# One row table per bin for all passes: surplus rows go on into the next pass's slots, and keys of paired groups are computed a step earlier

## The chip, the core and the metric

The kernel runs on one NeuronCore of a Trainium2 chip. A core has a matrix engine (TensorE, PE in the profile; its weight loads are PEld), a vector engine (VectorE, DVE), a scalar engine (ScalarE, ACT), a general engine (GpSimd, POOL) and a queue for transfers (SyncE, SP). Each runs its own list of instructions in order and waits for the others by semaphores. Tiles lie in on-chip memory of 128 partitions (SBUF), products of PE in PSUM, and everything large in the device's DRAM. The metric is the device time of one execution, in microseconds.

## What is computed

The reference is a layer of a graph network with 12,500 nodes (N), 400,000 edges (E) and 128 features:

```
h   = relu(layernorm(x))                     # N x 128
hin = h @ W_in2f.T
Wij = smu(f @ W_f1.T + b_f1) @ W_f2.T + b_f2 # E x 128, from 20 edge attributes
Wij = Wij * edge_weight[:, None]
x_ij = hin[dst] * Wij                        # one message per edge
agg = segment_sum(x_ij, src, N)              # messages added up by node
out = x + smu(agg @ W_o1.T + b_o1) @ W_o2.T + b_o2
```

`smu(v)` is a smooth bend of v (a linear part and an erf part), done with a GELU table. The edges are sorted by `dst`, so a run of edges reads few rows of `hin`; `src` is random, so the sum by `src` is a scatter.

## The kernel before

**Tiles, groups, passes.** 128 edges make a tile, 4 tiles a group (`GRP`), 2 groups a super-tile. There are 782 groups, and a step of the main loop stands for one of them. The groups are cut into ten passes (`PARTS`, called epochs in the code). The nodes are cut into 98 bins of 128.

**A group's way.** PE makes the hidden layer (`hide`, line 918), ACT bends it (`bend`, 926), PE weighs it (`weigh`, 998 and 1000). PE gathers rows of `hin` with a one-hot matrix (`gather`, 954), ACT scales them by the edge weights (`take`, 973), and DVE multiplies both (`mix`, 1040, or 1031 for a paired group) into a message tile `ms`, of which there are nine. Beside it, the place of every message in its bin is counted: DVE marks bins (671 to 725), PE counts with triangular matrices (`count`, 752), DVE takes the maximum (`read`, 796) and writes the row numbers `ix` (`number`, 818). Then POOL sends the tile, one indirect DMA per 128 rows, to a table in DRAM (`scatter_rows`, 1110). A row has 128 values and a last one that says which node of the bin it is for; in the last value the round of the table is also written (`mark`, 1088), so that older rows left in a table don't count.

**Paired groups.** In some groups tiles 2 and 3 are matched with tiles 0 and 1, and a matched pair is written as one double row. `number` writes `key` (812); PE spreads the keys (`spread_keys`, 830), DVE compares (`match`, 838), PE ranks what is left over (`rank_left`, 848 and 849), DVE turns the ranks into a selection (`place_left`, 855 and 856), PE permutes (`permute`, 875) and ACT copies (898, 899). Left-over rows go out with a later group, the host (`bins`, lines 724 and 725; `number`, line 821).

**Tables and sums.** Each pass fills a table with a fixed number of slots per bin (`CAP`, a multiple of 128 that the largest bin is to fit into). While pass k fills its table, the table of pass k-1 is read back and summed: SP fetches two or more bins into `rw` (`fetch`, 1141), DVE builds one-hot selections (`choose`, 1155), PE multiplies block by block of 128 rows (`add`, 1168), and ACT or DVE adds the result into `agg` (1180, 1182). The blocks per bin are CAP/128: 6, 6, 6, 6, 5, 4, 3, 3, 2, 1, together 42. The sums begin seven steps into a pass (`LANDED`). Three DRAM buffers serve the ten tables in turn (`BUFS`). Before a buffer's first use its slots above a safe minimum (`ZMIN`) are set to zero by SP (`clear`, 226), spread over the pass in front: table 0 in the first 50 groups, table 1 in the rest of pass 0, table 2 in pass 1.

**Order.** The order of PE, DVE, ACT and SP is written out by hand in the main loop (`tc.manual_schedule`). A step holds, in this order: `send`, leftovers of a timetable, `number` of the next group, `weigh`, half of the sums (`parts`), `spread_keys`, `mix`, `permute`, `match`, `gather` and `take` for the step after, `hide`, `bend`, `take_pairs`, `count`, `pick_part`, `number_left`, `bins`, `read`, the other half of the sums, `rank_left` and `place_left`. `load` asks SP for a super-tile's inputs three super-tiles ahead. `chores` issues the clears and fetches of a step. If a bin overflows its table, a flag sends the kernel into a second, plain path at the end.

Of the kernel before, what the change touches and what calls it, by code (L numbers as in the profile page):

```python
# [9 lines left out]
F32 = mybir.dt.float32  # L10
# [22 lines left out]
PARTS = (59, 58, 58, 58, 47, 37, 27, 24, 16, 7)  # L33
EVERY = (3,) + (2.5,) * 7
UNPAIRED = 10
FIRST_PAIRED = 50
LATE_OF = 1, 3
LATE_FREE = 6
# [3 lines left out]
BUFS = 3  # L42
SIGMA = 4.6
ROW = P + 1
BIG = 2047.0
ZP = 128
ROUND = 12582912.0
NOBIN_ROW = float(1 << 17)
# [3 lines left out]
def gnn_kernel(  # L52
# [45 lines left out]
    CAP, ZMIN = [], []  # L98
    for a, n in eps_of:
        last_groups = UNPAIRED / (SUP // GRP)  # L100
        paired = n - last_groups if 0 < len(CAP) < len(eps_of) - 1 else 0
        if not CAP:
            paired = max(0, n - last_groups - FIRST_PAIRED / (SUP // GRP))
        late_one = len(CAP) >= len(eps_of) - SENT_LAST
        every = LATE_OF[1] / LATE_OF[0] if late_one else EVERY[len(CAP)]
        if late_one and paired:
            paired = n - LATE_FREE / (SUP // GRP)
        mean = (n + WIDER * paired / every) * SUP * P * P / N
        dev = SIGMA * math.sqrt((n + 2 * WIDER * paired / every) * SUP * P * P / N)
        CAP.append(math.ceil((mean + dev) / P) * P)  # L110
        ZMIN.append(max(0, math.floor((n * SUP * P * P / N - dev) / ZP) * ZP) if len(ZMIN) < BUFS else 0)
    assert all(c <= CAP[k % BUFS] for k, c in enumerate(CAP)) and (EPOCHS - 1) // BUFS < GRP
    Q = [c // P for c in CAP]
    ROWS = 2 * max(Q)
    SPAN = [ROWS // q for q in Q]
    assert all(NB * c + P + max(CAP) + 2 * int(BIG) < NOBIN_ROW and c < BIG - 1 for c in CAP)
# [8 lines left out]
    SPILL = P + int(BIG) + max(CAP)  # L125
    SPILLS = 3
    stores = [dram.tile([NB * CAP[k] + SPILLS * SPILL, ROW], F32, name=f"buf{k}") for k in range(min(BUFS, EPOCHS))]
    bufs = [stores[k % BUFS][0:NB * CAP[k], :] for k in range(EPOCHS)]
    wide = [stores[k % BUFS][0:NB * CAP[k] + SPILLS * SPILL, :] for k in range(EPOCHS)]
# [50 lines left out]
    bad = const.tile([P, 5 + 2 * EPOCHS], F32, name="bad")  # L180
# [27 lines left out]
    spot = const.tile([P, 2], F32, name="spot")  # L208
    drow = const.tile([P, SPILLS * EPOCHS], F32, name="drow")

    CB = 2
    zero = const.tile([ZP, CB * max(c - z for c, z in zip(CAP[:BUFS], ZMIN)) * ROW // ZP], F32, name="zero")
    cleans = [(b, n) for b, n in chunks(NB - 1, CB)] + [(NB - 1, 1)]

    def clear(k, c, engine):

        b, n = cleans[c]
        if b == NB - 1:
            m = CAP[k] * ROW // ZP
            rows = bufs[k][b * CAP[k]:(b + 1) * CAP[k], :].rearrange("(p s) r -> p (s r)", p=ZP)  # L220
            for o, w in chunks(m, zero.shape[1]):
                engine.dma_start(rows[:, o:o + w], zero[:, :w])
            return None
        m = (CAP[k] - ZMIN[k]) * ROW // ZP
        rows = bufs[k][b * CAP[k]:(b + n) * CAP[k], :].rearrange("(b c) r -> b c r", c=CAP[k])[:, ZMIN[k]:, :]
        return engine.dma_start(rows.rearrange("b (p s) r -> p b (s r)", p=ZP),
                                zero[:, :n * m].rearrange("p (b m) -> p b m", b=n))


# [119 lines left out]
    with tc.tile_pool(name="ld", bufs=4) as ld, \  # L349
# [213 lines left out]
        pair_no = {g: i for i, g in enumerate(list(paired) + late_pairs)}  # L563
        more_met = down.bitcast(F16)
# [123 lines left out]

        def bins(g):
# [21 lines left out]
            if g in first:  # L711
                nc.vector.memset(before, 0.0)
# [30 lines left out]
        def count(g):  # L743
# [17 lines left out]
            else:  # L761
# [4 lines left out]
                if lot is not None:  # L766
                    part(pc[:, n], tri, lot)
                    part(pc[:, n], ones_h, since[:, 2], stop=True)
# [1346 lines left out]
```

## Time and profile before

| | |
|---|---|
| median of three runs | 3832.49 us (3823.35 to 3832.53) |
| profiled execution | 3826.85 us |
| its span, first to last instruction | 3825.1 us |
| mean granted clock of TensorE | 0.964 |
| moved by DMA | 905.06 MB, 237 GB/s |

The page of the profile gives, for each engine, the time in which it was busy and its share of the span; a chain of waits, followed back from the last instruction; and groups of equal instructions, each with line, engine, operation, what it writes and reads, count, busy time, mean time of one, and the idle time of the engine in front of them with what ended it. Other views ask the same trace by line, by stretch of time, or by who waited for whom: there, "A <- B: t, n, m" says that A waited for B for t us in n cases, at most m at once. "issue" is time in which the engine waited for nothing that the profile shows. Stretches are given in us from the span's start; in each, the busy time of an engine has the count of its instructions behind it, followed by the granted clock, the busy share of the 16 DMA engines and GB/s.

### The profile page before, as it was taken

What the parts mean: (1) busy time and instruction counts of PE and PEld (TensorE: products, weight loads), DVE (VectorE), ACT (ScalarE), POOL (GpSimd) and SP (SyncE); (2) the same over time, 40 slices, a digit from 0 to 9 for tenths busy, and PEclk for the clock granted to TensorE, in tenths of its full rate; (3) what the DMA queues carried; (4) which work ended last, traced back from release to release, by engine and by line L of the source; (5) the groups of instructions that cost most, each with busy time, mean ns of one, the idle gap of its engine ahead of it and who ended that gap; (6) DMA issues with size and microseconds to landing.
All of it is one profiled execution on the core that took longest, in us unless ns stands there. A gap on an engine that the chain in (4) does not pass through costs nothing.

```text
span 3825.1 us, 90354 instructions
## 1 busy us (share of the span) xinstructions
PE 3294.2 (86%) x28066; PEld 2872.9 (75%) x28066; DVE 3116.8 (81%) x8275; ACT 2839.2 (74%) x7986; POOL 2855.5 (75%) x2946
## 2 busy tenths in 40 slices
PE   8777776988888999999989889999999889997767
PEld 4346665877777888878878778888888888887657
DVE  7878976877777888888888888888898888886657
ACT  7767766878888888888888888888778777875102
POOL 6777777777767777777777777777777777777776
PEclk9989988999999999999999999999999999999889
DMA  5888888888888878888878878888888888886977
GB/s 156 231 236 239 236 230 233 248 251 246 263 253 232 238 227 231 244 239 235 229 222 232 235 214 242 253 239 247 232 244 249 233 235 246 241 236 177 312 247 228
DMA packets 663936, 905.06 MB, mean 237 GB/s; under 512 B 179875, under 2 KB 462631, under 8 KB 663321
## 3 DMA queue, kind: packets, MB, share of 16 engines
q1 hardware_dynamic: 556025, 666.99, 63.5%
q0 software_dynamic: 100112, 219.93, 17.8%
q10 hardware_dynamic: 7312, 12.29, 0.9%
q8 instruction: 228, 3.74, 0.4%
q14 instruction: 259, 2.12, 0.2%
HBM read 500.66 MB, written 398.23 MB: 235 GB/s over the span
## 4 chain that ended last, share of the span: by engine, by line
PE 33%; DMA 18%; DVE 16%; ACT 11%; issue 11%; POOL 9%; SPq 2%; ACTq 0%; DVEq 0%; POOLq 0%
DMA buf<-ms,ix 12%; PE pg L1168 10%; POOL buf L1110 9%; PE pw L998 6%; PE pt L875 5%; ACT hg L973 3%; PE pc L752 3%; DVE se L1155 3%; DVE mt L838 2%; DVE ms L1040 2%; ACT oh L634 2%; ACT ge L926 2%; PE ph L954 2%; PE pw L1000 1%; DVE pc L796 1%
## 5 line engine op out<-in xcount | busy, mean ns | idle before, releaser
L1110 POOL DMA_INDIRECT buf<-ms,ix x2516 | 2444.3, 971 | 813.6 <-issue 569.0
L1168 PE MATMUL pg<-se,rw 128*128 128x128 f32 x8036 | 1168.7, 284 | 107.8 <-DVE se L1155 61.2
L1168 PEld LDWEIGHTS pg<-se,rw 128*128 128x128 f32 x8036 | 1037.2, 194 | 166.4 <-issue 65.5
L973 ACT ACTIVATE hg<-ph,w_sb 128x128 f32<-128x128 f32 x2784 | 781.9, 361 | 94.5 <-PE ph L954 80.4
L998 PE MATMUL pw<-w_f,ge 128*128 128x128 f32 x5568 | 779.2, 284 | 30.5 <-DVE ms L1040 14.3
L998 PEld LDWEIGHTS pw<-w_f,ge 128*128 128x128 f32 x5568 | 697.5, 197 | 50.0 <-issue 23.7
L1155 DVE TENSOR_TENSOR se<-irow_ps,rw 128x1536 f32<-128x1536 f32 (+1 forms) x345 | 587.4, 1703 | 112.1 <-DMA rw<-buf 89.5
L634 ACT ACTIVATE oh<-rbc,nrow 128x512 bf16<-128x512 uint8 x725 | 538.6, 743 | 33.5 <-DMA rbc<-rel_dram 33.1
L635 ACT ACTIVATE oh<-oh,onesb 128x512 bf16<-128x512 bf16 x743 | 536.0, 721 | 24.2
L796 DVE TENSOR_REDUCE pc<-pc 128x4 f32<-128x392 f32 (+1 forms) x782 | 466.4, 596 | 81.0 <-PE pc L752 77.4
L1040 DVE TENSOR_TENSOR ms<-pw,hg 128x512 f32<-128x512 f32 x482 | 330.2, 685 | 137.8 <-DMA buf<-ms,ix 36.5
L875 PE MATMUL pt<-ms,mt 128*128 128x129 f32 x2676 | 345.0, 279 | 55.0 <-DVE at L855 48.2
L875 PEld LDWEIGHTS pt<-ms,mt 128*128 128x128 f32 x2676 | 319.1, 193 | 66.7 <-issue 23.3
L752 PE MATMUL pc<-eo,tri 128*128 128x392 f16 x782 | 261.5, 334 | 69.8 <-DVE ix L818 46.8
L954 PE MATMUL ph<-hw,oh 126*128 126x128 bf16 x2784 | 274.4, 221 | 39.0 <-ACT hg L973 36.0
L926 ACT ACTIVATE ge<-pu 128x512 f32<-128x512 f32 x451 | 272.9, 605 | 17.4 <-PE pu L918 15.5
L752 PE MATMUL pc<-so,ones_h 128*128 128x392 f16 (+1 forms) x996 | 279.4, 306 | 0.1
L1000 PE MATMUL pw<-wls,f 128*128 128x128 bf16 x2784 | 274.2, 222 | 0.0
L1088 ACT ACTIVATE ms<-lo_b,mark 128x4 f32<-128x4 uint8 x309 | 91.3, 295 | 231.9 <-DVE ms L1040 219.7
L1110 POOL DMA_INDIRECT buf<-lt,ix x214 | 203.3, 950 | 78.0 <-issue 27.7
L954 PEld LDWEIGHTS <-oh 126*128 126x128 bf16 x2784 | 217.0, 99 | 52.5 <-issue 44.3
L752 PEld LDWEIGHTS <-ones_h 128*128 128x128 f16 x1554 | 151.8, 98 | 139.2 <-issue 17.1
(344 smaller groups left out, 5313.0 us busy)
## 6 DMA issues: line engine op xcount, KB each, us to landing
rw<-buf SPq DMA_DIRECT2D x292, 774.0 KB
f<-f_parts SPq DMA_DIRECT2D x370, 240.0 KB
buf<-zero SPq DMA_DIRECT2D x146, 387.0 KB
rbc<-rel_dram SPq DMA_DIRECT2D x389, 128.0 KB
buf<-ms,ix POOLq DMA_INDIRECT x2516
f_parts<-hs SPq DMA_DIRECT2D x105, 360.0 KB
rw<-buf SPq DMA_DIRECT2D x49, 645.0 KB
f_parts<-hs SPq DMA_DIRECT2D x107, 240.0 KB
```

The lines of the kernel that those rows point to most:

```text
L634: nc.scalar.activation(oh, loaded[s][1][:, o:o + n], AF.Abs, bias=pneg if s < FEW // SUP else nrow)
L635: nc.scalar.activation(oh, oh, AF.Relu, scale=-1.0, bias=onesb[:, 0:1])
L752: nc.tensor.matmul(to, by, of, start=start, stop=stop, skip_group_check=True)
L796: nc.vector.tensor_reduce(sl[:, :n], pc[:, :n], op=ALU.max, axis=AX.X)
L875: nc.tensor.matmul(po[:, j * (ROW + 1):j * (ROW + 1) + w], pp[:, o:o + P], ms[:, i, ROW:ROW + w], start=(i == 0), stop=(i == 1))
L954: nc.tensor.matmul(ph[:, j * P:(j + 1) * P], oh[:3 * WIN, a:a + P], hw[:3 * WIN, g % PER, :], start=True, stop=True)
L973: nc.scalar.activation(hg[:, j * P:(j + 1) * P], rows_of[g][:, j * P:(j + 1) * P], AF.Copy, scale=w_sb[:, t + j:t + j + 1])
L998: nc.tensor.matmul(pw[:, a:a + P], ge[:, a:a + P], w_f2, start=(a == 0), stop=False, skip_group_check=True)
L1040: nc.vector.tensor_tensor(ms[:, :n, 0:P], pw.rearrange("p (j f) -> p j f", f=P)[:, :n], hg.rearrange("p (j f) -> p j f", f=P)[:, :n], op=A ...
L1110: i = nc.gpsimd.indirect_dma_start(out=(wide if g in host or g in pair_no else bufs)[k][:, :], out_offset=bass.IndirectOffsetOnAxis(ap=ix, ...
L1155: nc.vector.tensor_tensor(se[:, a:a + n], own.unsqueeze(1).to_broadcast([P, n, P]), rows_in[c][:, a:a + n, P:P + 1].to_broadcast([P, n, P] ...
L1168: nc.tensor.matmul(pgs[0][:, g, :], rows_in[c][:, o, 0:P], sel[c][:, o, :], start=(q == 0), stop=(q == Q[k] - 1))
```

## The change

1. **One table for all passes.** Each bin has one stretch of S = 3200 rows in one DRAM tile, `store`. Pass k writes at `OFF[k]` in it. Passes 0 to 4 form a chain of five tables, 5 to 7 one of three, 8 and 9 stand alone (`CHAINS`). A bin that has more rows than `CAP[k]` goes on into the slots of the next pass's table, up to `LIM[k]`, and the next pass starts its counts with that surplus (`carry`, formed by a product with `one_h` at the end of a pass). Only the last table of a chain must hold the largest sum. The blocks per bin become 5, 5, 5, 5, 5, 4, 3, 3, 2, 1, together 38. The passes get other lengths (`PARTS`).
2. **Clears.** All five tables of the first chain are cleared above `ZMIN`, each in the first three quarters of the pass in front (`by_group`), from 64 partitions in place of 128. Pieces are at most three rows of 64 partitions and two bins, so tables 3 and 4 take two pieces where the others take one. Chains 2 to 4 lie over tables already read.
3. **Waits.** The dependences between scatters, fetches and clears are declared by hand: a pass's first fetch waits for all its scatters; scatters wait for the clears of the tables of their own and earlier passes, and, past three quarters of a pass, for those of the next; pass 5 waits for the fetches of tables 0 to 2.
4. **Keys.** `number` of a paired group moves from the start of the step before its `mix` to the end of the step in front, right after `read`.
5. **Ranks.** `spot` is negated and added on PE by a product with `ident` in `rank_left`; `place_left` compares the sum in PSUM with `falling`, a row of negative numbers, and line 855 falls away. In `bins`, two operations of a host become one, and its count uses `rest_h`.
6. Two kinds of message tile replace views of one; in `mix`, ACT's copy of keys is written after DVE's product.

```
-PARTS = (59, 58, 58, 58, 47, 37, 27, 24, 16, 7)
+PARTS = (58, 55, 54, 53, 48, 42, 33, 25, 16, 7)
+CHAINS = (5, 3, 1, 1)
-SIGMA = 4.6
+SIGMA = 4.5
-ZP = 128
+ZP = 64
...
+    for i, n in enumerate(CHAINS):
+        a = len(CAP)
+        ends = [0]
+        for k in reversed(range(a, a + n)):
+            ends.insert(0, max(ends[0] + 1, math.ceil(sum(rows_for(k, a + n)) / P)))
+        caps = [(u - v) * P for u, v in zip(ends, ends[1:])]
...
+    store = dram.tile([NB + SPARE, S, ROW], F32, name="buf")
+    rows_at = store.rearrange("b s r -> (b s) r")
...
+        z = 0 if b == NB - 1 else ZMIN[k]
+        m = (CAP[k] - z) * ROW // ZP
+        rows = store[b:b + n, OFF[k] + z:OFF[k] + CAP[k], :].rearrange("b (p s) r -> p b (s r)", p=ZP)
+        out = []
+        for o, w in chunks(m, zero.shape[1] // n):
+            out.append(engine.dma_start(rows[:, :, o:o + w], zero[:ZP, :n * w].rearrange("p (b m) -> p b m", b=n)))
+        return out
...
             if g in first:
-                nc.vector.memset(before, 0.0)
+                if carried(first[g]):
+                    nc.vector.tensor_scalar(before, carry, BIG, None, op0=ALU.min)
+                else:
+                    nc.vector.memset(before, 0.0)
...
-                    nc.vector.tensor_scalar(lot, bin_row, left_of[host[g]][1], None, op0=ALU.is_equal)
-                    nc.vector.tensor_add(then, whole, lot)
+                    lot = then
+                    nc.vector.scalar_tensor_tensor(then, bin_row, left_of[host[g]][1], whole, op0=ALU.is_equal, op1=ALU.add)
...
+                if carried(k + 1):
+                    on_one = bank_of[:, 1, :NB]
+                    nc.tensor.matmul(on_one, one_h, after, start=True, stop=True)
+                    nc.vector.tensor_scalar(carry, on_one, -float(CAP[k]), 0.0, op0=ALU.add, op1=ALU.max)
...
-            nc.tensor.matmul(at_, tri, met_of(g, 0, 2), start=True, stop=False, skip_group_check=True)
+            nc.tensor.matmul(at_, ident, spot, start=True, stop=False, skip_group_check=True)
+            nc.tensor.matmul(at_, tri, met_of(g, 0, 2), start=False, stop=False, skip_group_check=True)
...
-            at_ = cnt.tile([P, 2], F32, name="at")
-            nc.vector.tensor_tensor(at_, spot, kt[:, 2 * P:2 * P + 2], op=ALU.subtract)
             nc.vector.tensor_tensor(pp[:, 4 * P:].rearrange("p (j e) -> p j e", j=2),
-                                    irow_ps.unsqueeze(1).to_broadcast([P, 2, P]),
-                                    at_.unsqueeze(2).to_broadcast([P, 2, P]), op=ALU.is_equal)
+                                    falling.unsqueeze(1).to_broadcast([P, 2, P]),
+                                    kt[:, 2 * P:2 * P + 2].unsqueeze(2).to_broadcast([P, 2, P]), op=ALU.is_equal)
...
+                for j in range(FIRST):
+                    if (j == 0 and g >= BY) or 0 < j <= k or (j == k + 1 and is_clean(g)):
+                        behind_all(i, after_clear[j])
+                    else:
+                        apart(i, f"cleared{j}")
...
+        by_group = {k: eps_of[k][0] * PER + eps_of[k][1] * PER * 3 // 4 for k in range(FIRST - 1)}
...
-            elif k + 1 < BUFS:
+            elif k + 1 < FIRST and cleared < len(cleans):
                 past = BY if k == 0 else 0
-                upto = min(len(cleans), -(-(i + 1 - past) * len(cleans) // (ng - 4 - past)))
+                upto = min(len(cleans), -(-(i + 1 - past) * len(cleans) // (by_group[k] - g0 - 2 - past)))
                 while cleared < upto:
-                    clear(k + 1, cleared, nc.sync)
+                    cleared_rows(k + 1, cleared)
                     cleared += 1
...
             step()
-            number(at(p + 1))
+            if at(p + 1) not in paired:
+                number(at(p + 1))
             weigh(at(p + 1))
...
             read(at(p + 2))
+            if at(p + 2) in paired:
+                number(at(p + 2))
             parts(hi)
```

More of the change, by code (lines that the diff above doesn't have):

```diff
@@ L97, in gnn_kernel @@
     EPOCHS = len(eps_of)
[L98 to L111, printed above, removed]
@@ L1073, in send @@
             t, n = groups[g]
[L1074 removed]
+            ms = message_tile()
             places_in(g, ms)
@@ new lines, in gnn_kernel, with is_clean, behind_all, apart @@
+        sent = [[] for _ in range(EPOCHS)]
+        after_clear = [[] for _ in range(FIRST)]
+        after_fetch = [[] for _ in range(EPOCHS)]
+        def is_clean(g):
+            k = epoch[g // PER]
+            return k + 1 < FIRST and g > by_group[k]
+        def behind_all(i, names):
+            for name in names:
+                tc.add_manual_dep(i.ins, name, AFTER, reason="rows of a table")
+            names.clear()
+        def apart(i, others):
+            tc.declare_no_dep(i.ins, group=others, reason="slots are disjoint")
```

166 lines of the change are left out of this document (98 added, 68 removed).

## The prediction

> **What bounds the kernel now.** The page's busy shares come first. They put TensorE (PE) ahead and GpSimd (POOL) only level with the rest, and the chain of waits gives POOL 9%:
>
> ```profile
> PE 3294.2 (86%) x28066; PEld 2872.9 (75%) x28066; DVE 3116.8 (81%) x8275; ACT 2839.2 (74%) x7986; POOL 2855.5 (75%) x2946
> PE 33%; DMA 18%; DVE 16%; ACT 11%; issue 11%; POOL 9%; SPq 2%; ACTq 0%; DVEq 0%; POOLq 0%
> ```
>
> Both mislead here. POOL does one thing, the scatters of line 1110, and the groups by form and the instructions of that line show its real load:
>
> ```profile
> L1110 POOL DMA_INDIRECT buf<-ms,ix x2516 | 2444.3, 971 | 813.6 <-issue 569.0 <-DMA buf<-ms,ix 54.0 <-ACT ms L1090 39.9
> L1110 POOL DMA_INDIRECT buf<-lt,ix x214 | 203.3, 950 | 78.0 <-issue 27.7 <-DVE ix L821 16.6 <-DVE pc L796 4.6
> L1110 POOL DMA_INDIRECT buf<-ms,ix_kept x163 | 158.3, 971 | 49.7 <-issue 45.7 <-DMA buf<-ms,ix_kept 2.1 <-ACT ms L898 0.3
> L1110 POOL DMA_INDIRECT buf<-ge,ix x9 | 8.8, 979 | 2.7 <-issue 1.8 <-DMA w_sb<-in_x 0.3 <-ACT ms L1806 0.3
> ...
> L1110 POOL DMA_INDIRECT buf<-ms,ix x2516: 952/958/1520, 13.0 to 3544.0; - x194
> L1110 POOL DMA_INDIRECT buf<-ms,ix_kept x163: 954/958/1352, 3545.2 to 3763.6; - x163
>   issue: 644.3, 2111
> ```
>
> 2902 scatters take 2814.7 us. Ahead of each lies a gap that waits for nothing, 644.3/2111 = 0.305 us; for all, 885 us. Begun at 13.0, such a run without any other wait ends at 13.0 + 2814.7 + 885 = 3713. The last scatter begins at 3763.6 and so ends near 3764.5. **POOL loses only some 52 us to waits in the whole run**; behind it lies a tail of 61 us to the span's end, 3825.1. Where the 52 us lie, POOL's waits show, asked for 0 to 100, 100 to 600, 600 to 680 and 680 to 1200 us, then for 1200 to 3500. Below them stand the engines' busy times in stretches of 500 us, and the product that line 782 makes at the end of each pass:
>
> ```profile
> POOL buf L1110 <- ACT ms L1078: 7.7, 12, 2.2
> ...
> POOL buf L1110 <- ACT ms L1090: 14.5, 15, 3.4
> ...
> POOL buf L1110 <- DVE ix L821: 6.9, 2, 4.7
> ...
> POOL buf L1110 <- ACT ms L1090: 22.7, 14, 5.1
> POOL buf L1110 <- DVE ix L821: 7.6, 4, 4.0
> ...
> POOL buf L1110 <- ACT hg L973: 13.2, 42, 0.6
> ...
> L782 PE MATMUL ph<-so,ones_h x10: 203/203/242, 595.5 to 3674.4; 128*128 128x98 f16 x10
> ```
> ```profile
> core 0: us, PE busy (x) PEld busy (x) DVE busy (x) ACT busy (x) POOL busy (x), PEclk, DMA share, GB/s
> 100.00:600.00 500.00, 365.09 (x2489) 264.49 (x2488) 411.44 (x1265) 350.69 (x1001) 371.72 (x379) 0.90 0.83 233
> 700.00:1200.00 500.00, 434.57 (x3824) 387.79 (x3823) 390.42 (x1045) 408.94 (x1166) 364.29 (x376) 0.97 0.88 253
> 1200.00:1700.00 500.00, 457.42 (x4108) 407.71 (x4107) 427.84 (x1142) 431.20 (x1236) 380.15 (x394) 1.00 0.83 235
> 1700.00:2200.00 500.00, 452.01 (x4017) 403.06 (x4015) 422.24 (x1137) 424.48 (x1194) 379.77 (x393) 0.99 0.81 229
> ```
>
> With the gap of 0.305 taken off each, the five named waits are 4.0, 9.9, 6.3, 18.4 and 6.4 us, 45 in all: 14 in pass 0, which ends with the first product of line 782 at 595.5 us, and 31 in pass 1. From 1200 us on POOL runs scatter behind scatter, 394 and 393 in 500 us. **From there no work taken off PE, DVE or ACT moves the end.** The change can win what POOL loses before 1200 us, and scatters that fall away.
>
> **The change, part by part.**
>
> *Scatters.* Each paired group makes three scatters of four. By the code's rule 224 groups are paired in place of 223, since the passes have other lengths: 2901 scatters, 0.970 + 0.305 = 1.3 us gained.
>
> *Blocks, 42 to 38 per bin.* Tables 0 to 3 lose one each (6 to 5), summed in passes 1 to 4; tables 4 to 9 keep theirs.
>
> ```profile
> L1168 PE MATMUL pg<-se,rw 128*128 128x128 f32 x8036 | 1168.7, 284 | 107.8 <-DVE se L1155 61.2
> L1155 DVE TENSOR_TENSOR se<-irow_ps,rw 128x1536 f32<-128x1536 f32 x292 | 511.0, 1750 | 107.3 <-DMA rw<-buf 87.7 <-PE pg L1168 18.9 <-DMA rbc<-rel_dram 0.3
> L1155 DVE TENSOR_TENSOR se<-irow_ps,rw 128x1280 f32<-128x1280 f32 x49 | 72.6, 1482 | 4.8 <-PE pg L1168 2.8 <-DMA rw<-buf 1.8
> ```
>
> Two records make one block product, so a block costs PE 1168.7/4018 = 0.291 us. 98 bins lose 28.5 us in each of passes 1 to 4, 114 in all; DVE's selections lose 49 x 0.268 = 13 us a pass. In passes 2 to 4 this only makes PE wait longer for free message tiles. In pass 1 it falls on the path.
>
> *Keys at the end of the step in front.* The spreading transposes wait for line 812 (whole run, then 700 to 1200 us):
>
> ```profile
> PE pt L830 <- DVE key L812: 70.9, 63, 6.3
> ...
> PE pt L830 <- DVE key L812: 10.9, 9, 6.3
> ```
>
> The key is moved on DVE ahead of the second part of the sums and of place_left, which begin 0.16 us later; on PE up to 10.9 us fall away in pass 1. What is late next is the match, which then waits for its own transposes.
>
> *Smaller work on DVE, a product more on PE.*
>
> ```profile
> L724 DVE TENSOR_SCALAR el<-mv,lat 128x98 f16<-128x98 f32 x214 | 65.5, 306 | 0.3
> L725 DVE TENSOR_TENSOR so<-so,el 128x98 f16<-128x98 f16 x214 | 45.5, 213 | 7.3
> L1843 DVE SCALAR_TENSOR_TENSOR so<-mv,lat,so 128x98 f16<-128x98 f32 x8 | 2.6, 321 | 0.3
> L855 DVE TENSOR_TENSOR at<-spot,pt 128x2 f32<-128x2 f32 x214 | 32.0, 150 | 4.6 <-PE pt L849 4.0
> L849 PE MATMUL pt<-met,ones_h 128*128 128x1 f16 x192 | 31.3, 163 | 0.0
> ```
>
> Lines 724 and 725 become one form that line 1843 shows (0.519 to 0.321 us), and line 855 goes (0.150 us): 0.35 us for a paired group, 12 us of DVE in pass 1's 35. For it PE gets ident by spot, a float32 product of two columns that the trace doesn't show. Two records of L1168's rate (0.145) are 0.29 us, two of its mean (0.284) 0.57; I take 0.33, two of L849, as nearest in width: 11 us in pass 1. It can start before the match ends. The f16 row in place of the PSUM row in the comparison of line 856 I take at no change. The extra checks and the carry are a few operations of line 855's size, once or twice a pass.
>
> PE in pass 1 then loses 28.5 + 10.9 - 11 = 28 us (20 to 39), about the 31 that POOL lost there.
>
> *Clears and loads.* Tables 0 to 2 clear 192 rows of a bin, not 384; tables 3 and 4, new, 256 each, all written within the first three quarters of a pass, in 64-partition pieces, and for tables 3 and 4 two pieces per pair of bins. SP issues 349 clears in place of 149:
>
> ```profile
> L226 SPq DMA_DIRECT2D buf<-zero x147: 377/447/3212, 47.4 to 1139.6; - x147
> ```
>
> Bytes, with rows of 516: a table's clear over 98 bins falls from 19.6 to 9.9 MB in passes 0 and 1, and passes 2 and 3 get 13.1 each where they had none; fetches lose 6.5 MB in each of passes 1 to 4. Pass 1 moved 253 GB/s against 235 after it (the stretches above). Pass 2 lasts 399 scatters of 1.275 = 509 us, its clearing part 382; there it rises by 13.1 MB/382 us = 34 less 12 of the fetches, to 257 GB/s. Pass 1 falls by some 9 and 12 to 232: **what pass 1 bore moves there.**
>
> *New waits on POOL.* The first scatter past three quarters of a pass waits for the next table's clears, with all later scatters behind it. They are issued two groups earlier, SP runs ahead by three super-tiles of loads, and POOL lags: I take zero. If that cover is gone it costs up to four landings; the longest in the chain of waits is the first row here, the second is DVE's, in order of time:
>
> ```profile
> 142.84 10.55 DMA buf<-zero
> ...
> 645.90 1.76 DVE L1155 TENSOR_TENSOR se<-irow_ps,rw 128x1536 f32<-128x1536 f32 x1 [8.58 <-DMA rw<-buf]
> ```
>
> The second is the start of the sums in pass 1: the first fetch lands late, DVE stands 8.58 us, and POOL's 6.3 us follow. The change leaves this order, though the last quarter of pass 0 is now free of clears.
>
> **Sum.** Pass 1: of some 10 us at its start (6.3 and a wait of 4) I take 5 back, of the other 21 I take 15. Pass 0: 0, from -5 to +5, since its clears have half the bytes but a table's 49 now go out in 35 groups, not 64. Passes 2 and 3: 5 us of new waits, since the transfers are as dense as in old pass 1 while PE has less to do. Together -5 - 15 + 5 - 1.3 = -16 us. The profiled execution took 3826.85 us, 1.75 beyond its span and 5.6 below the median of the three runs, 3832.49. From the median: **3816 us**; this case's own range is 3800 to 3824.
>
> **Rivals.**
>
> *All waits go.* If pass 1 was bound by PE alone, the 45 us go and the new passes stay covered: 3832.5 - 46 = 3786. For it: 28 us less on PE there. Against it: the late first fetch, and transfers on the chain. It is also where a reader of the chain, who counts 114 us of products and 70.9 of key waits, is stopped by POOL. Chance 0.12.
>
> *No change.* Pass 1 waits for loads rather than PE. Loads stand in 700 to 1200 us thus:
>
> ```profile
> ACT oh L634 <- DMA rbc<-rel_dram: 11.1, 5, 7.0
> PE pu L918 <- DMA f<-f_parts: 5.5, 1, 5.5
> ```
>
> If these, and not PE, emptied the message tiles, halved clears return some 8 us and passes 2 and 3 take 5 of them: 3828. The clock could do the same: granted 0.90 at 100 to 600 us beside 365 us of PE, 1.00 at 1200 to 1700 beside 457. If less work in pass 1 brought it from 0.97 to 0.94, PE's 435 - 28 = 407 us there would grow by 13 and give back half. The Trainium skill, "TensorE: Matmul & The Clock Gate", section "What's actually happening", states that an idle window of about 3.4 us halves the clock; by that rule thinner work favours this rival, but the trace has 1.00 beside an idle PE of 43 us in 500, so I give it little. Chance 0.25.
>
> *Slower: SP falls behind in passes 2 and 3.* SP is one queue for clears, fetches and every load. Its waits are its slack (700 to 1200 us, then 1200 to 1700):
>
> ```profile
> SPq L1141 <- PE pg L1168: 19.5, 6, 5.9
> ...
> SPq L1141 <- PE pg L1168: 53.3, 19, 6.0
> SPq L1141 <- PE pt L849: 13.2, 7, 3.9
> SPq L604 <- ACT oh L634: 13.1, 11, 6.5
> ```
>
> At least 79.6 us of 500 without clears, 61 in the 382 us in which a pass clears. 99 clears of 0.447 us fit (44 us). Beyond 61/99 = 0.62 us each they don't. At 1.0 us, loads run 38 us late in each pass, and with the 21 us won before: 3832.5 - 21 + 76 = 3888 at worst, 3858 if the nine message tiles absorb 15 in each. For it: clears up to 3.212 us. Against it: they are half as large, and PE is lighter. The Trainium skill, "DMA: Bandwidth & Descriptors", section "Rules for kernel authors", asks for large transfers over all partitions, and calls those under 64 KB mostly overhead; the one-row pieces, 66 KB from 64 partitions, are what it warns of. No run yet shows such a piece. Chance 0.12.
>
> *The tables overflow.* Then the flag sends the kernel into its slow second path, and the time leaves this scale. The limits keep 4.5 deviations: chance 0.01.
>
> **How the numbers follow.** Forecast 0.50, all gone 0.12, no change 0.25, slower 0.12, overflow 0.01. A measurement tells about 0.3% (11.5 us) from no change. Below 3821 lie four fifths of the forecast and all of the first rival: 0.52. Within 0.3%: a tenth of the chances from the forecast, nearly all of no change: 0.35. Slower: 0.13. For 8 in 10 the range runs from 3786 to 3844.
>
> **What would show it.** Right: POOL's busy time in 700 to 1200 us at 378 or more, line 830 without key waits, 7252 records of line 1168 in place of 8036, and the last scatter 16 us sooner with the same tail. Wrong: waits of POOL above 0.3 us beyond 1200 us, SP's waits near zero in passes 2 and 3, POOL waiting for a clear, or a tail that changes. If POOL's gap or scatter time itself moved, the floor would.

## The result, and the profile after

The changed kernel takes **3854.93 us** (median of four runs, 3851.51 to 3856.58) beside 3831.08 us before (3823.35 to 3832.53): 1.0068 times the time before, 95% interval 1.0055 to 1.008. It is 0.7% slower, where 16 us less were forecast. The profiled execution took 3854.62 us with a span of 3852.9, 27.8 more than before.

The page's busy shares and chain, the scatters by form, and the instructions of their line (duration in ns, lowest, median and highest; first and last start in us). Line 1110 is now line 1133:

```profile
PE 3262.0 (85%) x27445; PEld 2856.5 (74%) x27758; DVE 3012.7 (78%) x7859; ACT 2814.7 (73%) x7992; POOL 2870.3 (74%) x2946
PE 31%; DMA 21%; DVE 18%; ACT 10%; issue 10%; POOL 9%; SPq 2%; DVEq 0%; ACTq 0%; POOLq 0%; another core or an unknown queue 0%
```
```profile
L1133 POOL DMA_INDIRECT buf<-ms,ix x2514 | 2456.1, 977 | 836.5 <-issue 549.8 <-DMA buf<-ms,ix 53.7 <-ACT ms L1113 41.4
L1133 POOL DMA_INDIRECT buf<-lt,ix x215 | 205.6, 956 | 69.3 <-issue 30.3 <-DVE ix L849 5.7 <-DVE so L736 4.3
L1133 POOL DMA_INDIRECT buf<-ms,ix_kept x163 | 158.8, 974 | 49.7 <-issue 45.1 <-DMA buf<-ms,ix_kept 3.1 <-DMA rw<-buf 0.6
...
L1133 POOL DMA_INDIRECT buf<-ge,ix x9 | 8.5, 941 | 2.7 <-issue 2.1 <-DMA rw<-buf 0.3 <-ACT agg L1255 0.3
```
```profile
L1133 POOL DMA_INDIRECT buf<-ms,ix x2514: 953/962/1941, 13.2 to 3572.9; - x194
...
L1133 POOL DMA_INDIRECT buf<-ms,ix_kept x163: 955/961/1442, 3574.1 to 3792.6; - x163
```

Less is busy on PE and DVE, as the change meant, and the span is longer all the same. The prediction's own sum tells where. 2901 scatters now take 2829.0 us, and with the gap of 0.305 each a run without other waits would end at 13 + 2829 + 885 = 3727; it was 3713. The last one ends at 3793.6, so POOL loses 67 us, not 52. The tail behind it stays (59.3, was 60.6). Of the 28 us more, **14 are dearer scatters and 15 are waits**.

The waits have moved. POOL's, asked for 360 to 600 and for 1200 to 2100 us, and the engines' busy times by stretches:

```profile
POOL buf L1133 <- issue: 50.3, 122, 4.0
POOL buf L1133 <- ACT ms L1113: 8.4, 5, 4.9
POOL buf L1133 <- ACT rw L289: 4.6, 1, 4.6
...
POOL buf L1133 <- issue: 151.8, 465, 3.7
POOL buf L1133 <- ACT ms L1113: 27.8, 17, 4.0
...
POOL buf L1133 <- DVE ix L849: 6.9, 11, 1.7
```
```profile
100.00:600.00 500.00, 375.15 (x2591) 278.20 (x2591) 413.44 (x1260) 357.01 (x1024) 364.13 (x367) 0.90 0.75 201
700.00:1200.00 500.00, 434.49 (x3776) 390.21 (x3828) 381.69 (x1009) 412.52 (x1183) 380.15 (x394) 0.96 0.85 238
1200.00:1700.00 500.00, 429.71 (x3727) 383.71 (x3778) 384.14 (x1004) 399.74 (x1151) 366.75 (x377) 0.97 0.86 235
1700.00:2200.00 500.00, 436.23 (x3838) 388.85 (x3890) 400.79 (x1047) 405.68 (x1166) 367.08 (x379) 0.98 0.88 242
```

POOL waits longer for late message tiles (line 1113) in pass 0, and between 1200 and 2100 us, where none of its waits had been longer than 0.7 us. The two rows `issue`, which name nobody, hold 13 and 10 us beyond 0.305 for each gap. Twelve of their gaps are longer than 0.5 us, and in eleven of these the scatter starts 0.75 us after DVE's product in `mix` (line 1063) has ended, so they are late message tiles as well. POOL's busy time in 700 to 1200 us rose from 364 to 380, back to back; in 1200 to 2200 it fell from 380 to 367 in each 500 us. The transfers did not get as dense there as forecast: 235 and 242 GB/s, where 257 were expected.

The next rows are the clears, the first row of SP's waits in 1200 to 1700 us, and ACT's wait in the whole run for the loads of `rbc`, from which it makes the one-hot matrix `oh` of the gather. This last wait was 33.1 us in 14 cases before:

```profile
L237 SPq DMA_DIRECT2D buf<-zero x349: 485/652/2812, 48.0 to 2035.5; - x175
```
```profile
SPq L1200 <- PE pg L1227: 15.7, 9, 3.9
...
ACT oh L644 <- DMA rbc<-rel_dram: 93.5, 37, 9.4
```

A clear now has at most half the bytes and takes 0.652 us to issue in place of 0.447. SP's first row there was 53.3 us; all rows of the view together fall from 115 to 51 us, and in 1700 to 2200 us from 120 to 37. So SP still waits now and then, but it has much less to spare, and what it loads comes late.

### The profile page after: what moved, and what is told of

Read it like the earlier page. It is cut to its first block, busy times and chain, and to the rows that moved or that the text cites. A ratio compares the mean times of both kernels' runs of the same rounds, so it can differ in the third digit from the quotient of the medians.

```text
span 3852.9 us, 89322 instructions
## 1 busy us (share of the span) xinstructions
PE 3262.0 (85%) x27445; PEld 2856.5 (74%) x27758; DVE 3012.7 (78%) x7859; ACT 2814.7 (73%) x7992; POOL 2870.3 (74%) x2946
## 4 chain that ended last, share of the span: by engine, by line
PE 31%; DMA 21%; DVE 18%; ACT 10%; issue 10%; POOL 9%; SPq 2%; DVEq 0%; ACTq 0%; POOLq 0%; another core or an unknown queue 0%
DMA buf<-ms,ix 14%; POOL buf L1133 9%; PE pg L1227 7%; PE pw L1025 6%; PE pt L902 5%; ACT hg L1000 3%; PE pc L767 3%; DMA rbc<-rel_dram 3%; DVE mt L866 2%; DVE pc L824 2%; DVE ms L1063 2%; DVE se L1214 2%; ACT oh L644 2%; PE pw L1027 2%; PE ph L981 1%
## 5 line engine op out<-in xcount | busy, mean ns | idle before, releaser
L1227 PE MATMUL pg<-se,rw 128*128 128x128 f32 x7252 | 1087.1, 286 | 109.0 <-DVE se L1214 61.7
L1227 PEld LDWEIGHTS pg<-se,rw 128*128 128x128 f32 x7252 | 954.2, 195 | 164.6 <-issue 59.1
L1025 PE MATMUL pw<-w_f,ge 128*128 128x128 f32 x5568 | 788.7, 286 | 44.6 <-DVE ms L1063 27.3
L1214 DVE TENSOR_TENSOR se<-irow_ps,rw 128x1280 f32<-128x1280 f32 (+1 forms) x345 | 535.4, 1552 | 128.3 <-DMA rw<-buf 101.9
L644 ACT ACTIVATE oh<-rbc,nrow 128x512 bf16<-128x512 uint8 x726 | 540.2, 744 | 93.5 <-DMA rbc<-rel_dram 93.5
L902 PE MATMUL pt<-ms,mt 128*128 128x129 f32 (+1 forms) x2688 | 356.0, 284 | 45.4 <-DVE mt L883 19.8
L902 PEld LDWEIGHTS pt<-ms,mt 128*128 128x128 f32 x2688 | 328.8, 197 | 58.4 <-issue 23.9
L953 ACT ACTIVATE ge<-pu 128x512 f32<-128x512 f32 x450 | 273.5, 608 | 16.7 <-PE pu L945 16.3
L767 PE MATMUL pc<-so,ones_h 128*128 128x392 f16 x782 | 261.2, 334 | 0.0
L681 DVE TENSOR_TENSOR eo<-irow_ps,ed 128x784 f16<-128x784 f16 (+1 forms) x391 | 216.9, 555 | 25.9 <-ACT ed L671 25.6
L1027 PEld LDWEIGHTS <-f 128*128 128x128 bf16 x2784 | 222.0, 101 | 9.8
```

What stands on the lines that cost most here:

```text
L644: nc.scalar.activation(oh, loaded[s][1][:, o:o + n], AF.Abs, bias=pneg if s < FEW // SUP else nrow)
L767: nc.tensor.matmul(to, by, of, start=start, stop=stop, skip_group_check=True)
L902: nc.tensor.matmul(po[:, j * (ROW + 1):j * (ROW + 1) + w], pp[:, o:o + P], ms[:, i, ROW:ROW + w], start=(i == 0), stop=(i == 1))
L1025: nc.tensor.matmul(pw[:, a:a + P], ge[:, a:a + P], w_f2, start=(a == 0), stop=False, skip_group_check=True)
L1027: nc.tensor.matmul(pw[:, a:a + P], fb[:, o + a:o + a + P], wls, start=False, stop=(a + P == n), skip_group_check=True)
L1214: nc.vector.tensor_tensor(se[:, a:a + n], own.unsqueeze(1).to_broadcast([P, n, P]), rows_in[c][:, a:a + n, P:P + 1].to_broadcast([P, n, P] ...
```

## The experiments

For each run with a comparable profile this table gives what the scatters of its trace show, in us: how much longer than 0.305 the gaps between scatters were, by stretch of the span, and the mean duration of a scatter. It is worked out as the prediction's sum was, from start and end of every scatter; there is one profile for each kernel. Every ratio below is to the kernel before on the same chip.

| | 0-600 | 600-1200 | 1200-2200 | waits in all | mean scatter | span |
|---|---|---|---|---|---|---|
| before | 19.6 | 31.3 | 0.7 | 52 | 0.9699 | 3825.1 |
| after | 31.0 | 0.2 | 36.3 | 67 | 0.9752 | 3852.9 |
| keys and ranks alone | 20.2 | 28.9 | 0.8 | 50 | 0.9749 | 3835.4 |
| tables alone | 26.5 | 0.0 | 28.3 | 55 | 0.9716 | 3829.4 |
| clears from ACT | 40.2 | 0.0 | 63.5 | 104 | 0.9728 | 3882.5 |
| half clears, old tables | 95.7 | 64.3 | 6.2 | 166 | 0.9712 | 3941.4 |
| whole clears | 24.1 | 1.0 | 0.6 | 26 | 0.9737 | 3807.4 |
| whole clears, old keys | 21.5 | 0.9 | 4.2 | 27 | 0.9742 | 3810.2 |
| whole clears, old keys and ranks | 18.3 | 0.0 | 0.0 | 18 | 0.9739 | 3800.2 |
| whole clears, old ranks | 16.7 | 0.8 | 0.0 | 17 | 0.9746 | 3801.3 |

Some runs fell on chips on which the kernel before itself took some 5650 us (medians of 5647 to 5716), with POOL waiting in every stretch; their times say little of this bound, and they stand together below.

### The two halves of the change

Keys and ranks alone, with the one operation for a host, on the tables of before:

```
-            number(at(p + 1))
+            if at(p + 1) not in paired:
+                number(at(p + 1))
...
+            nc.tensor.matmul(at_, ident, spot, start=True, stop=False, skip_group_check=True)
...
-            at_ = cnt.tile([P, 2], F32, name="at")
-            nc.vector.tensor_tensor(at_, spot, kt[:, 2 * P:2 * P + 2], op=ALU.subtract)
```

> The kernel before with the keys at the end of the step in front, the ranks with the added product, and one operation for a host; tables, clears and blocks stay as before. Theory Q (the loss comes from the many clears that SP issues, and from scatters 5 ns dearer, both belonging to the new tables): POOL's stalls in pass 0 and beyond 1200 us stay as before (20 and 1 us), the mean scatter stays at 0.970 us, and of the 31 us of stalls in pass 1 some 10 to 25 go: 3806 to 3821 us. Rival K (the moved keys or the ranks delay something in passes 0, 2 and 3): the eight stalls of pass 0 and those of 1200 to 2100 us appear here too: 3850 us or more. Rival B (pass 1 was eased by the lighter sums or the halved clears, not by the keys): stalls in pass 1 stay near 31 us: 3826 to 3832.

Measured: 3833.72 us, 1.0002 (0.9986 to 1.0018). Pass 1 keeps its waits, 28.9 of 31.3: this is rival B, to within 2 us. Neither the loss of rival K nor the gain hoped for from the keys is there.

The tables alone, with keys and ranks as before (the same lines, undone in the changed kernel; the one operation for a host stays):

> The changed kernel with the keys and the ranks of before; tables, clears and blocks as changed. Theory Q: the stalls of pass 0 and passes 2 and 3 are all here, and pass 1 keeps part of its stalls: 3855 to 3875. Rival K: without the moved keys the stalls go: 3815 to 3830. If the lighter sums and clears alone ease pass 1, 600 to 1200 us shows less than 10 us of stalls here too.

Measured: 3842.98 us, 1.0036 (1.0023 to 1.0049). The lighter sums and the clears of pass 1 end all its waits by themselves, and the new waits in pass 0 and in 1200 to 2200 us are here. Theory Q's places hold; its time was set too high, since keys and ranks turn out to cost, not to win: the change with them is at 1.0068.

### Who issues the clears, and in what pieces

```
-            for i in clear(k, c, nc.sync):
+            for i in clear(k, c, nc.scalar):
```

> The changed kernel with the clears issued by ScalarE's queue in place of SP's; the same pieces, the same bytes. Theory Q: SP gets 228 us (349 of 0.652) back, its waits return to 50 us or more in 1200 to 1700 us, and the 60 us of stalls of POOL in pass 0 and in passes 2 and 3 fall below 25, unless ACT, busy 80%, cannot bear 65 us more in a pass: 3800 to 3830. Rival D (the bytes of the clears crowd the loads, whoever issues them): stalls stay, 3850 to 3860. The mean scatter stays at 0.975 us by both.

Measured: 3891.94 us, 1.0167 (1.0137 to 1.0197), slower than both theories expected. The rows are the clears, SP's first wait and POOL's wait for the tiles in 1200 to 1700 us, and ACT's wait for `rbc` in the whole run:

```profile
L237 ACTq DMA_DIRECT2D buf<-zero x349: 477/583/2042, 50.2 to 2062.2; - x175
```
```profile
SPq L1200 <- PE pg L1227: 64.8, 20, 7.8
...
POOL buf L1133 <- ACT ms L1113: 31.6, 19, 4.2
...
ACT oh L644 <- DMA rbc<-rel_dram: 5.4, 3, 3.5
```

With the very same pieces `rbc` is waited for 5.4 us in place of 93.5, and SP has its slack again. This row alone doesn't settle why, since ACT, which waits for `rbc`, is late itself here. The loads' own time does. For those that ACT waited for, the median from issue to the end of the wait was 7.1 us in the changed kernel (37 loads), 7.5 before (14), 8.0 here (3), and 8.4 with the whole clears below (18). So the loads of the changed kernel did not travel longer; SP issued them late. It was SP's time, then, and not that the bytes or the width of the clears slowed the loads. But ACT has no such time either: it now finishes the tiles late itself, and the issue time is the same debt in another queue. The Trainium skill, "DMA: Bandwidth & Descriptors", section "Issuing engines are not separate DMA queues", states that starting transfers on several engines saves only the sequencer's time, usually small beside the transfer. The trace agrees that SP's time is saved (64.8 us of waits in place of 15.7), and here that small part decided.

Then the pieces: all 128 partitions, three bins in one issue, from row 384 of a bin on.

```
-ZP = 64
+ZP = 128
...
-    CB = 2
-    zero = const.tile([P, CB * 3 * ROW], F32, name="zero")
+    CB = 3
+    zero = const.tile([P, CB * 2 * ROW], F32, name="zero")
```

> The changed kernel with clears of 128 partitions, two rows wide and three bins each, from row 384 of each bin on for every table: about 165 issues in place of 349, and 18% more bytes cleared (1280 rows of a bin in place of 1088). Theory Q: with half the issues the 60 us of stalls fall by half or more: 3805 to 3830. Rival D (bytes): stalls the same or larger, 3855 to 3865.

Measured: 3812.10 us, 0.9955 (0.9939 to 0.9972). 18% more bytes and 43 us less than the changed kernel: theory Q, and rival D is out. The rows are the clears, SP's and POOL's first waits of 1200 to 1700 us, and ACT's in the whole run:

```profile
L237 SPq DMA_DIRECT2D buf<-zero x169: 384/445/3402, 47.3 to 1981.9; - x169
```
```profile
SPq L1200 <- PE pg L1227: 34.1, 15, 8.0
...
POOL buf L1133 <- issue: 81.1, 266, 0.3
...
ACT oh L644 <- DMA rbc<-rel_dram: 31.5, 18, 6.1
```

An issue over 128 partitions is back at 0.445 us although it carries twice the bytes of the narrow one. POOL's longest gap in that stretch is the ordinary 0.3.

The counterpart: the kernel before, its tables untouched, with each clear as two issues of 64 partitions.

```
-        return engine.dma_start(rows.rearrange("b (p s) r -> p b (s r)", p=ZP),
-                                zero[:, :n * m].rearrange("p (b m) -> p b m", b=n))
+        for half in chunks(CAP[k] - ZMIN[k], (CAP[k] - ZMIN[k]) // 2):
+            out.append(engine.dma_start(rows[:, half[0]:half[0] + half[1], :].rearrange("b (p s) r -> p b (s r)", p=ZP // 2),
+                                 zero[:ZP // 2, :n * m].rearrange("p (b m) -> p b m", b=n)))
```

> The kernel before with each clear split into two issues of 64 partitions, once more, since the first time the chip took 5653 us for the kernel before and POOL stood still in every part of it. Theory Q: stalls of POOL grow by 20 to 30 us in pass 0 and by 10 to 30 in pass 1, none beyond 1200 us: ratio 1.006 to 1.015. Rival D (only bytes count): ratio 0.998 to 1.002.

Measured: 3940.54 us, 1.0282 (1.0263 to 1.0301). The waits come where Q puts them, beside the clears: 76 us more in the first 600 us, three times what was expected, and 33 up to 1200. The clears' line, then POOL's and ACT's waits of 100 to 600 us:

```profile
L228 SPq DMA_DIRECT2D buf<-zero x294: 529/651/1883, 47.1 to 1255.3; - x147
```
```profile
POOL buf L1113 <- ACT ms L1093: 63.5, 21, 9.7
...
ACT oh L637 <- DMA rbc<-rel_dram: 59.2, 14, 7.9
...
POOL buf L1113 <- ACT ms L1081: 31.8, 23, 9.0
```

SP got 147 x 0.65 + 147 x 0.20 = 125 us more to issue, and the kernel lost 110. How much of SP's time passes on depends on what it has to spare: between the narrow and the whole clears it was 43 us of 349 x 0.652 - 169 x 0.445 = 152. This run changes width and number of the issues at once; it alone doesn't tell them apart.

### Keys or ranks

With whole clears, three kernels undo one or both of them: `number` at its old place (old keys), the rank lines of before (old ranks), or both.

> Changed tables, clears of 128 partitions and three bins, keys and ranks of before, once more for the same reason. Theory R (moved keys or changed ranks make scatters dearer): ratio 0.993 to 0.994 where whole clears with both changes had 0.9955, mean scatter near 0.971. Rival N (the mean of one execution only varies so much): ratio 0.9955.

> As the run in front with the changed ranks, the keys at their old place, once more. Theory R with the keys as cause: ratio 0.993 to 0.994 and a mean scatter near 0.971; with the ranks as cause: 0.9955 and 0.974. Rival N: 0.9955 with either mean.

> As the two in front with the keys moved and the ranks of before, once more. Theory R with the keys as cause: ratio 0.9955, mean scatter near 0.974; with the ranks as cause: 0.993 to 0.994, near 0.971. Rival N: 0.9955 with either mean.

| whole clears, with | us | ratio, 95% interval |
|---|---|---|
| new keys, new ranks | 3812.10 | 0.9955 (0.9939 to 0.9972) |
| old keys, new ranks | 3812.55 | 0.9952 (0.9938 to 0.9965) |
| old keys, old ranks | 3801.43 | 0.9921 (0.9908 to 0.9934) |
| new keys, old ranks | **3800.20** | **0.9917 (0.9903 to 0.9930)** |

The first row comes from another chip than the other three. The ranks cost 0.0031 to 0.0038 of 3830, some 13 us, the keys nothing either way. The cause that theory R gave has fallen: the mean scatter is 0.974 to 0.975 in all four. The waits differ, 26 and 27 us against 18 and 17, which is 8 to 9 of the 13; where the rest lies these single profiles don't show. The last of the four, with whole clears, the moved keys and the ranks of before, beats both kernels.

What the new ranks delay shows in the groups of PE and DVE, with whole clears: first the new ranks, then the old ones:

```profile
L876 PE MATMUL pt<-spot,ident 128*128 128x2 f32 x430 | 75.2, 245 | 61.7 <-DVE mt L866 60.2
L876 PEld LDWEIGHTS pt<-spot,ident 128*128 128x128 f32 x430 | 67.8, 197 | 86.2 <-DVE mt L866 82.1 <-issue 2.6
L877 PEld LDWEIGHTS <-tri 128*128 128x128 f16 x224 | 41.9, 187 | 0.0
```
```profile
L875 PE MATMUL pt<-met,tri 128*128 128x2 f16 x192 | 32.1, 167 | 56.4 <-DVE mt L865 54.7 <-issue 0.6
L882 DVE TENSOR_TENSOR at<-spot,pt 128x2 f32<-128x2 f32 x215 | 31.9, 148 | 2.6 <-PE pt L876 2.5
...
L875 PEld LDWEIGHTS <-tri 128*128 128x128 f16 x224 | 23.0, 103 | 3.1 <-issue 3.0
```

The product needs nothing of the match, yet its first weight load waits for it, 82.1 us in all. Before, PE had `tri` loaded while it waited and only the product stood behind. From the match's end to the comparison the old way takes 0.167 + 0.164 + 0.148 = 0.48 us, the new one 0.197 + 2 x 0.245 + 2 x 0.164 = 1.02 (an estimate, from means of these rows and of line 878, 0.164): half a microsecond for each of 224 paired groups, some 120 us in all. Most of that is hidden; that it is the source of the 13 us is argued here, not shown.

### Runs on the slow chips

Each edit of these is told above, but for three: one bin per clear (`CB = 1`), four bins at 64 partitions, and the product moved to the end of `spread_keys`:

```
-            nc.tensor.matmul(at_, ident, spot, start=True, stop=False, skip_group_check=True)
...
+            nc.tensor.matmul(kt[:, 2 * P:2 * P + 2], ident, spot, start=True, stop=False, skip_group_check=True)
             matched[g] = kt
```

> The kernel before, with each clear split into two issues of 64 partitions (3 rows each, two bins: the very pieces of the changed kernel); same tables, same bytes, 294 issues in place of 147. Theory Q (the issue of such pieces on SP's queue makes loads late): some 125 us of SP's time more, 40 a pass; stalls of POOL grow by 20 to 30 us in pass 0 and by 10 to 30 in pass 1: 3850 to 3890. Rival D (only bytes count): 3825 to 3838. Rival P (64 partitions cost only because two pieces go where one went in passes 2 and 3, while PE is lighter there): pass 0 as before.

> The changed tables with clears of 128 partitions and three bins, but the keys and the ranks of before. Theory R (moved keys or changed ranks make scatters some 4 ns dearer on average, since DVE's work falls otherwise against POOL's: 41.6 and 45.2 us above 0.958 with the old ones, 52 to 56 with the new): the mean scatter falls from 0.9737 to about 0.971, 8 us: 3800 to 3806. Rival N (the mean of one execution only varies so much): 3812 as with the new ones.

> As the run in front, with the changed ranks but the keys at their old place. Theory R with the keys as cause: like the old ones, 3800 to 3806 and a mean scatter near 0.971. With the ranks as cause: 3810 to 3814 and 0.974. Rival N: 3812 with either mean.

> As the two in front, with the keys moved but the ranks of before. Theory R with the keys as cause: 3810 to 3814, mean scatter near 0.974. With the ranks as cause: 3800 to 3806, near 0.971. Rival N: 3812 with either mean.

> The kernel before with one bin per clear: 128 partitions, 294 issues in place of 147, the same bytes. Half clears of 64 partitions, as many and as large, cost 110 us. Theory C (the number of issues sets the loss): 3900 us or more, ratio above 1.02. Theory W (the loss comes from transfers over 64 partitions, which cost more to issue and to move): an issue stays near 0.45 us, 66 us more of SP in 1140: ratio 1.000 to 1.010.

> The kernel before with clears of 64 partitions over four bins: 147 issues as before, the same bytes for each. Theory C (number of issues): ratio 0.998 to 1.005. Theory W (64 partitions): an issue of 0.6 us or more, ratio above 1.015. If number and width both count, between them.

> The changed kernel with whole clears of three bins (ratio 0.9955), and the product of ident and spot moved from rank_left to the end of spread_keys, ahead of the match. Theory M (the ranks cost their 11 us because the product stands behind the wait for the match: line 876 waits for line 866, and its 0.5 us of PE and the load of tri, 187 in place of 100 ns, lie on the way from the match to the permuting): ratio 0.992 to 0.993 as with the old ranks. Rival T (PE's time for the product, 0.5 us a group, costs it wherever it stands): 0.995 to 0.996. Rival F (the comparison with falling is what costs): 0.995 to 0.996 as well, with line 876 no longer waiting.

> The changed kernel once more. Theory S (its scatters are dearer by 5 ns because of what it changes): mean again 0.975 and median 0.962. Rival N (this differs from execution to execution): mean 0.970 to 0.974 and median 0.958. The stalls come at the same places by both: 20 to 28 us in pass 0, 30 to 40 in 1200 to 2100 us, ratio 1.005 to 1.008.

| | ratio, 95% interval |
|---|---|
| half clears, old tables | 1.0036 (1.0010 to 1.0061) |
| one bin, twice | 1.0017 (0.9995 to 1.0040), 1.0046 (1.0010 to 1.0083) |
| half partitions | 1.0006 (0.9984 to 1.0027) |
| whole clears: early product, twice | 0.9956 (0.9935 to 0.9976), 0.9966 (0.9941 to 0.9991) |
| whole clears: old keys and ranks; old keys; old ranks | 0.9970, 0.9968, 0.9987, all within 0.9945 to 1.0015 |
| the changed kernel | 0.9991 (0.9965 to 1.0017) |

One bin and the early product ran a second time, on two more such chips:

> The kernel before with one bin per clear (128 partitions, 294 issues, the same bytes), once more, since the first time POOL stood still in every part of the kernel before as well (5656 us); that run showed the price, 0.43 us an issue over 128 partitions and 0.62 over 64, whatever their bytes. Theory I (loss follows SP's time in issuing): 147 x 0.45 = 66 us of SP's time more, where half clears had 147 x 0.65 + 147 x 0.20 = 125 us more and lost 110: ratio 1.008 to 1.016. Theory W (transfers over 64 partitions are what crowd the loads): 1.000 to 1.003.

> The changed kernel with whole clears of three bins and the product of ident and spot at the end of spread_keys, ahead of the match, once more: the first time POOL stood still in every part of the kernel before as well (5656 us), but it showed that the product no longer waits for the match there. With the product behind the match the ratio was 0.9955 and 0.9952, with the ranks of before 0.9921 and 0.9917. Theory M (place): 0.990 to 0.993. Rivals T (PE's time for the product) and F (the comparison with falling): 0.994 to 0.996.

On these chips the changed kernel takes as long as the one before. POOL's waits in the whole run of half clears say why these ratios can't decide between the theories: POOL lost time in every pass, to other engines that were late:

```profile
POOL buf L1113 <- DVE ix L824: 922.7, 178, 12.7
POOL buf L1113 <- issue: 770.4, 2341, 8.6
```

What they do show are prices and waits. The clears' lines of half clears, of one bin, and of half partitions:

```profile
L228 SPq DMA_DIRECT2D buf<-zero x294: 2/620/2104, 53.3 to 1622.9; - x147
```
```profile
L226 SPq DMA_DIRECT2D buf<-zero x291: 3/429/1797, 53.3 to 1638.4; - x146
```
```profile
L228 SPq DMA_DIRECT2D buf<-zero x150: 3/622/2204, 52.9 to 1596.0; - x150
```

64 partitions cost 0.62 us at 194 and at 387 KB, 128 partitions 0.43 at 194 KB. **For these clears the width sets the price of an issue, not the bytes.** And the early product:

```profile
L859 PEld LDWEIGHTS pt<-spot,ident 128*128 128x128 f32 x430 | 84.9, 245 | 1.6 <-issue 1.6
L859 PE MATMUL pt<-spot,ident 128*128 128x2 f32 x430 | 72.0, 237 | 1.2 <-issue 1.2
```

It no longer waits for the match. Whether that gives the 13 us back stays open. Its two ratios lie where rivals T and F expected them, but the old ranks were not faster on these chips either (0.9970 and 0.9987). The changed kernel's scatters had a median of 0.958 us here and a mean of 0.966. The median of 0.962 of its first profile was met here by two other kernels, one bin and the early product, and so isn't tied to the changed tables.

## Why the prediction was wrong

*What bounds the kernel* held: the span follows from POOL's scatters, its waits and the same tail in every profile of the table. 2901 scatters and 7252 records of block products came as counted.

*Clears and loads* is the step that failed, and in it the price of an issue. The forecast counted 349 issues, but at 0.447 us, and took their smaller size as a reason against a higher price; they took 0.652. That put 228 us on SP where 66 had been. The forecast's 5 us of new waits in passes 2 and 3 were 36. Pass 0, taken as 0 with 5 to either side, lost 11 more: there two tables are cleared, and SP had less to spare from the start (63 us of waits in 100 to 600, before). By the table some 4 to 7 of the 11 go with the keys and ranks (31.0 against 26.5, 24.1 against 16.7), in single profiles. That the narrow clears are the cause is shown both ways: whole clears take the 36 us away (0.6 left), and narrow ones, two in place of one, bring 110 us to the old kernel. The bytes were not what mattered, since 18% more of them ran 43 us faster, and the rows name no wait of POOL for a clear.

Of the 44 us between the forecast and the profile after, 30 lie in passes 2 and 3, 11 in pass 0 and 15 in the scatters; pass 1 won 11 more than forecast, and small differences take off the rest.

So the rival *SP falls behind*, which had 0.12, came true in its place and its mechanism. That its 3858 lies near the measured 3855 is luck: it was worked out for issues of 1.0 us, and at 0.652 the same sum makes loads only 65 - 61 = 4 us late in a pass and gives 3832.5 - 21 + 8 = 3820. Its point of decision, 0.62 us, is luck too: SP's rows came to 115 us of waits in 500, not 79.6, and after the change 51 and 37 us of them are left, yet loads are late. Slack in the sum of a stretch isn't slack at every load. What spoke against this rival, the smaller size, was the misreading; the nearest row, 0.447 for 128 partitions, was no bound for 64. The Trainium skill, "DMA: Bandwidth & Descriptors", section "Rules for kernel authors", which that rival cites, asks for all 128 partitions for the sake of bandwidth. That pointed the right way, though the reason in this kernel is SP's time; its line at 64 KB doesn't bear on most of these pieces (244 of 349 have 194 KB).

*Keys*: the waits for them fell, though not to nothing (line 830 is now 858; they were 70.9 us), and it won nothing:

```profile
PE pt L858 <- DVE key L840: 23.7, 25, 3.1
```

The step "on PE up to 10.9 us fall away in pass 1" is nearly true of PE (3.9 us are left in 700 to 1200 us), but pass 1 didn't hang on it: the tables alone took all 31 us there, of which 20 were forecast. That term was right in kind and too small. The clock's part in the rival *no change* did not come about: it was granted 0.96 in 700 to 1200 us, not 0.94, where it had 0.97. Nor does its fall to 0.97 in 1200 to 1700 us explain the new waits: with whole clears and old ranks it is 0.97 there too, and POOL loses nothing.

*Ranks*: "it can start before the match ends" was wrong in the order that was made; it waits. The new ranks cost some 13 us of the whole, where 11 us of PE in pass 1 were charged, and covered; how they cost it stays open. Its size, 0.33 us, was 0.49, within the bounds given. The comparison with `falling` went from 0.424 to 0.411 us: no change, as said.

*Scatter time itself* was named as what would move the floor, and had no price in the range. Scatters were 5 ns dearer in the profile after, 14 us. The means of the table run from 0.9699 to 0.9752, keys and ranks on the old tables have 0.9749 and the tables alone 0.9716, so the tables are not shown to be the cause; whole clears with old ranks are 30 us faster than before at 0.9746. What sets the mean stays open.

Taken one after the other, the ratios go as follows: the tables with whole clears and old ranks -0.0083, the new ranks +0.0038, clears from 64 partitions +0.0113: together +0.0068. The other way, over the tables alone, gives nearly the same sizes: 1.0036 - 0.9921 = 0.0115 for the clears, 1.0068 - 1.0036 = 0.0032 for keys and ranks.

## What to carry to other kernels

A queue that only issues transfers has a bound of its own: count its instructions in each stage with a measured price for their shape, and set that against its waits in that stage, as with any engine. Leave a margin: here loads were late while the queue still waited a tenth of the time. Fewer, wider issues can be worth more than fewer bytes. Handing issues to another engine that is busy itself moves the debt, it does not pay it. A product whose inputs are ready still waits where it is put in an engine's order: ask what stands in front of it.

## What the hardware showed

The price of issuing a clear hung on the partitions that it reads: 0.43 to 0.45 us for 128, 0.62 to 0.65 for 64, on both kinds of chip, at equal bytes (194 KB: one bin against half clears; 387 KB: the kernel before against half partitions).

Some chips, four by the record, took 5647 to 5716 us for a kernel that others run in 3830, with a granted clock near 0.82 in place of 0.96, scatters as long as elsewhere (median 0.958 to 0.962 us) and POOL's waits longer in every stretch. No run here says why.

Scatters that ran beside two subtractions of DVE were dearer. These are the main forms of the two lines, of the changed kernel:

```profile
L1706 DVE TENSOR_TENSOR hs<-sm,hs 120x512 bf16<-120x512 f32 x105 | 72.0, 686 | 7.7 <-ACT hs L1703 7.2 <-DMA buf<-zero 0.3
L1700 DVE TENSOR_TENSOR sm<-sm,hs 120x512 f32<-120x512 f32 x105 | 72.0, 685 | 10.7 <-ACT hs L1697 10.5
```

325 of the 2901 scatters overlap one of these lines in time; they take 1.054 us on average, the others 0.965 (before: some 326, with 1.031 and 0.962). That is 58% of what single scatters take above 0.958. No run took these lines away, so it is not shown that they are the cause.
